# A decoder on one core: in differential attention the next group's projections enter the queue of filling work a batch earlier, with a second buffer for turned tokens and a third for queries and keys

## The chip, the cores and the metric

The kernel runs on one core of a Trainium2 chip. The metric is the time of one execution in device microseconds (us); the time before is the median of three runs. The core has five engines that run side by side, each through its own list of instructions in order: TensorE (PE: matmuls, and the loading of their weights, PEld), VectorE (DVE), ScalarE (ACT), GpSimd (POOL) and SyncE (SP), which here only issues transfers (DMA). Semaphores tie the engines together.

## The reference, cut to what matters

Six layers follow each other on 8 batches of 256 tokens of width 512, each with a residual and a layer norm: differential attention, a long convolution gated by a context, a mixture of experts, self attention, cross attention, routed attention. The change lies in the first; its end touches the second.

```python
q = (x @ Wq.T).reshape(bsz, tgt, 2 * H, HD)          # H = 16, HD = 16
k = (x @ Wk.T).reshape(bsz, tgt, 2 * KVH, HD)        # KVH = 4
v = (x @ Wv.T).reshape(bsz, tgt, KVH, 2 * HD)
scores = jnp.where(causal, einsum(q, k) * scale, min)
probs = jax.nn.softmax(scores, axis=-1)
attn = attn1 - lambda_full * attn2                   # even and odd heads of probs @ v
attn = attn * rsqrt(mean(attn * attn) + EPS) * ln_w * (1.0 - LAMBDA_INIT)
x = layernorm(x + attn.reshape(...) @ Wo.T)
```

## The kernel before, in words

The 2048 tokens are 16 tiles of 128 (`x[0]` to `x[15]`), and four tiles make a group: two batches. `causal_attention` (L1220) runs the attention of three of the layers; only `diff_attention` (L286) hands it a function `gather` and 8 units a batch (`upb = 8`, L561; the others take `upb = 4`). So differential attention is a loop of 64 **units**, 16 to a group (`upg`), each a block of four rows of heads of one batch.

A unit `u` issues, in this order (L1497 to L1521):

- `maxima(u)`: 12 matmuls for plain scores (`ps_q`, L1280), a copy by ACT (`rows`, L1289), a causal mask by POOL (L1291); the row maxima by DVE (L1300) come at the unit's end;
- some filling work;
- `products(u - 10)`: weights times values and times ones (`ps_pv`, L1386 and L1396), a reciprocal by DVE (L1404), then `gather`, which subtracts the odd heads (L428);
- `weights(u - 9)`: scores again, turned, with the maxima added by a second matmul (`ps_k`, L1343 and L1352), the exponential by ACT (`pT`, L1360), a mask and a sum by POOL (L1361, L1371);
- more filling work. Once a batch `split` and `turn` make the maxima into a matmul's operand (`terms` on DVE, L1311; `ps_n` on PE, L1322).

`ps_q` and `ps_k` share one buffer of PSUM (`ps_sc`, one buffer, L1240).

**Filling work** is everything else that PE has to do: turning tokens (`pt<-ident,x`, L226, to `xT`), the projections to values (`ps_v`), keys (`ps_k<-xT`, to `kz`) and queries (`ps_f`, to `qT`), the norm of the heads (`ps_ss`, `pt_ss`, `pt_rr`) and the output projection (`ps_o`, with `res` and the layer norm behind it); all projections carry line 207, a helper's. It stands in a list of pieces with a due slot each, with costs in us written beside every step (`MM, TR = 0.86, 0.45`, L201). `begin(g)` asks `prepare` (L351) for the pieces of group `g` and puts them in with due slots from `16 * g` on, where the group's first unit needs them. `fill(budget)` takes steps from the head of the list until the budget is spent; `need(u + 1)` takes all that is due, whatever the budget; the budget of a unit is

```python
rate = max(2.4, pressure(u) + per_batch / upb)
...
if u % upg == upb and u // upg + 1 < NG:
    begin(u // upg + 1)
left = fill(left + rate - short - MM) - need(u + 1)
```

so group `g + 1` enters at the middle of group `g`, eight units before it is due, at units 8, 24 and 40. When the list is empty, a unit gets no filling. `prepare` also starts, for the last group, the loads of the context's tiles (`cx`), which are turned from unit 54 on and written back as `ctx_d` (L423 to L424).

The tiles of this layer come from the pool `a_work` on the left side of the core's memory (SBUF): `qT` (8,192 bytes a partition) and `kz` (4,096) in two buffers, `xT` (8,192) in one. In the program as it is built the pool lies at bytes 91,136 to 196,256 of every partition. Two large tiles of the next layer lie at the right: `first_h` at 163,808 to 196,576, in memory that the pool leaves, and `w_l1a` at 196,576 to 229,344, above the pool's end. `long_conv` (L566) keeps in the lower half of `first_h` the turned even tiles of tokens and in the upper half their context; `w_l1a` holds the same of the odd tiles, which are first used at half of its 32 steps (`h`). It loads the context from `ctx_d` (L582), turns tokens (L171, copied out at L121 and L123), loads a filter a step (`wt`, three buffers, L596), and multiplies (`ps_y`, L177: 20 matmuls a step). At step 2 it issues the experts' weights (`gu`, L709), three transfers of 2,816 KB, into memory that the tokens of the first layer leave when the last of them is turned. Outside the attention loops the order of instructions is a scheduler's, which places them by data and memory.

Of the kernel before, what the change touches and what calls it, by code (L numbers as in the profile page):

```python
# [17 lines left out]
F32 = mybir.dt.float32  # L18
# [6 lines left out]
P = 128  # L25
# [3 lines left out]
NG = NT // TPG  # L29
GT = TPG * P  # L30
KB = D // P
# [21 lines left out]
def decoder_kernel(ctx: ExitStack, tc: tile.TileContext, a: dict, out: bass.AP):  # L53
# [149 lines left out]
    def by_columns(ps, lhsT, rhs, start, stop):  # L203

        for s in range(4):
            cs = slice(32 * s, 32 * s + 32)
            nc.tensor.matmul(ps[cs], lhsT=lhsT[:, cs], rhs=rhs, start=start, stop=stop)  # L207

    def product_steps(tile, lhsT, rhs, done, cost=MM):

        ps = []

        def step(k):
            if k == 0:
                ps.append(tile())
            by_columns(ps[0], lhsT(k), rhs(k), k == 0, k == KB - 1)
            if k == KB - 1:
                done(ps[0])

        return [(cost, lambda k=k: step(k)) for k in range(KB)]  # L220

    def turned(pools, dst, src, tag="mm"):

        pt = pools.tile([P, KB, P], F32, tag=tag, name="pt")
        for k in range(KB):
            nc.tensor.transpose(pt[:, k, :], src[:, k * P : (k + 1) * P], ident)  # L226
        nc.scalar.copy(dst, pt)  # L227
# [20 lines left out]
    def turned_group(work, pools, g, bufs=1):  # L248

        xT = []  # L250

        def step(ti):
            if ti == 0:
                xT.append(work.tile([P, KB, GT], F32, tag="xT", name="xT", bufs=bufs))
            turned(pools, xT[0][:, :, ti * P : (ti + 1) * P], x[g * TPG + ti])

        return xT, [(0, [(TR, lambda ti=ti: step(ti))]) for ti in range(TPG)]
# [28 lines left out]
    def diff_attention():  # L286
# [62 lines left out]
        clear_slots(wpool)  # L349

        def prepare(work, pools, g, at, here):  # L351
            qT = work.tile([P, KB, GT], F32, tag="qT", name="qT")
            kz = work.tile([P, 2, GT], F32, tag="kz", name="kz")
            v = work.tile([P, TPG, P], F32, tag="v", name="v", bufs=3)
            xT, turns = turned_group(work, pools, g)
            batches = [slice(b * S, (b + 1) * S) for b in range(2)]

            def values(ti, ps=[]):
                if ti == 0:
                    ps.append(pools.tile([P, TPG, P], F32, tag="mm", name="ps_v"))  # L360
                for k in range(KB):
                    by_columns(
                        ps[-1][:, ti, :],
                        xT[0][:, k, ti * P : (ti + 1) * P],
                        wv[:, k, :],
                        k == 0,
                        k == KB - 1,
                    )
                if ti == TPG - 1:
                    nc.scalar.copy(v, ps.pop())  # L370

            values_steps = [(MM, lambda ti=ti: values(ti)) for ti in range(TPG)]

            def keys(tokens):
                def done(ps):
                    for i in range(2):
                        nc.scalar.mul(kz[:, i, tokens], ps, half[:, i : i + 1])

                n = tokens.stop - tokens.start
                return product_steps(  # L380
                    lambda: pools.tile([P, n], F32, tag="mm", name="ps_k"),
                    lambda k: wk[:, k, :],
                    lambda k: xT[0][:, k, tokens],
                    done,
                    MM * n / GT,
                )

            if g:

                need = turns + [(0, values_steps), (0, keys(slice(0, GT)))]  # L390
            else:
                need = turns[:2] + [(0, keys(batches[0]))]
                need += [(3, steps) for _, steps in turns[2:]]
                need += [(8, keys(batches[1])), (9, values_steps)]
            for b, tokens in enumerate(batches):
                for c, first in enumerate((0, 1, 4, 5)):
                    block = feature_block(pools, qT, xT, wq, 0, c, HD0**-0.5, tokens)
                    need.append((8 * b + first, block))
            need.sort(key=lambda piece: piece[0])

            if g == NG - 1:

                for t in range(2):
                    load_context(work, t)
                for t in range(NT):
                    slot = 16 * g + 6 + t
                    at(slot - here, "fill", [(TR, lambda t=t: turn_context(work, pools, t))])
            return (
                need,
                lambda rows, c, at, n: qT[rows, c // 4 * 2 + c % 2, at : at + n],  # L410
                lambda rows, c, at, n: kz[rows, c // 2 % 2, at : at + n],
                lambda k, h: v[:, k, 32 * (h % 4) : 32 * (h % 4) + 32],
            )
# [3 lines left out]
        def load_context(work, t):  # L417
            cx[t] = work.tile([P, D], F32, tag="cx", name="cx")
            nc.sync.dma_start(out=cx[t], in_=cin[:, t, :])

        def turn_context(work, pools, t):
            c = work.tile([P, KB, P], F32, tag="cT", name="cT")
            turned(pools, c, cx.pop(t))  # L423
            nc.sync.dma_start(out=ctx_d[:, :, t * P : (t + 1) * P], in_=c)  # L424
            if t + 2 < NT:
                load_context(work, t + 2)
# [793 lines left out]
    def causal_attention(name, prepare, finish, upb=KB, gather=None):  # L1220
# [18 lines left out]
        with ExitStack() as st:  # L1239
            work = st.enter_context(tc.tile_pool(name=f"{name}_work", bufs=2))  # L1240
            ps_sc = st.enter_context(tc.tile_pool(name=f"{name}_sc", bufs=1, space=PSUM))
            ps_pv = st.enter_context(tc.tile_pool(name=f"{name}_pv", bufs=1, space=PSUM))
            pools = st.enter_context(tc.tile_pool(name=f"{name}_ps", bufs=3, space=PSUM))
# [168 lines left out]
            upg = 2 * upb  # L1412
# [21 lines left out]
            def happen(place):  # L1434
                for f in events.pop((now[0], place), []):
                    f()
# [18 lines left out]
            def begin(g):  # L1455
                pieces, *groups[g] = prepare(work, pools, g, at, now[0])
                queue.extend((upg * g + slot, steps) for slot, steps in pieces)
                queue.sort(key=lambda piece: piece[0])
# [14 lines left out]
            def pressure(u):  # L1473

                total = most = 0.0
                begun = [(due[0], current)] if current and due[0] < units + 99 else []
                for slot, steps in begun + queue:
                    total += sum(c for c, _ in steps)
                    most = max(most, total / max(1, slot - u))
                return most  # L1480
# [16 lines left out]
            for u in range(units + lag + 2):  # L1497
                now[0] = u
                happen("start")

                rate = max(2.4, pressure(u) + per_batch / upb)
                if u < units:
                    largest = maxima(u)
                    short = max(0.0, min(0.8, rate - 1.8))
                    if rate > 2.7:
                        short += (rate - 2.7) / 2
                    left = fill(left + short)
                    sums(u)
                    happen("mid")
                    if u >= wait:  # L1510
                        weights(u - wait)
                    if u % upg == upb and u // upg + 1 < NG:
                        begin(u // upg + 1)
                    left = fill(left + rate - short - MM) - need(u + 1)

                    if u and u % upb == 0:
                        turn(u // upb - 1)
                    left = fill(left + MM)
                    largest()
                    if u % upb == upb - 1:  # L1520
                        split(u // upb)  # L1521
                else:

                    if u < units + wait:
                        weights(u - wait)
                    sums(u)
                    happen("mid")
                    left = fill(left + rate) - need(u + 1)
                    if u == units:
                        turn(B - 1)  # L1530
                happen("end")
# [7 lines left out]
    def feature_block(pools, r, xT, w, at, c, scale=1.0, tokens=slice(0, GT)):  # L1539

        cs = slice(at + c * P, at + (c + 1) * P)
        n = tokens.stop - tokens.start
        return product_steps(
            lambda: pools.tile([P, n], F32, tag="mm", name="ps_f"),
            lambda k: w[:, k, cs],
            lambda k: xT[0][:, k, tokens],
            lambda ps: nc.scalar.mul(r[:, c, tokens], ps, scale),
            MM * n / GT,
        )
# [722 lines left out]
```

## Time and profile before

| what | value |
|---|---|
| median of 3 runs | 2106.0 us (2105.93 to 2106.16) |
| the profiled execution | 2125.86 us, its span 2124.1 us |
| PE busy over the span | 1946.4 us, 92% |
| DVE, POOL, ACT busy | 58%, 40%, 29% |
| differential attention | from the start to about 470 us: the last layer norm ends at 469.8 us |
| first unit, last unit (first `ps_q`) | 13.6 us, 391.4 us |
| long convolution, first `ps_y` | 480.1 us |

The profile is of one execution and slower than the median by 20 us; all times within a stage are read from it. In its timeline a row is a start, a duration, an engine, a line, an operation, output and inputs, shapes and a count, and in brackets how long the engine sat idle before it and what ended that. A matmul of the program is two rows of the trace here, since the numbers are in float32. The length of a unit is read as the time from its first `ps_q` to the next unit's.

### The profile page before, as it was taken

The numbers are of one execution on the slowest core, as the hardware profiler recorded it, in microseconds if no ns is written. First come the engines' busy times: TensorE is split into PE (matmuls) and PEld (weight loads), VectorE is DVE, ScalarE is ACT, GpSimd is POOL, SyncE is SP. The second block draws the span as 40 slices with busy tenths as digits, with TensorE's granted clock in tenths as the row PEclk, the third lists the DMA queues.
The fourth block names the chain that finished last, engine by engine and source line by source line (L and its number), as shares of the span: only waits on it lengthen the run. The fifth ranks groups of instructions, "written<-read, shape, count | busy, mean of one in ns | idle before, by whom it ended". The sixth has DMA issues, their size and how long they took to land. (4 is left out here: it accounts for less than half of the span.)

```text
span 2124.1 us, 46456 instructions
## 1 busy us (share of the span) xinstructions
PE 1946.4 (92%) x20164; PEld 1130.5 (53%) x20164; DVE 1234.4 (58%) x1890; ACT 615.2 (29%) x787; POOL 853.3 (40%) x945
## 2 busy tenths in 40 slices
PE   7979999879998999999969999998999999888885
PEld 5545545434443445566535554545877876254443
DVE  4677777658888974122226757556334342437877
ACT  4555555520010012111114343430101102144442
POOL 2677777637556823000015645343000000216663
PEclk9999999999999999999989999999999999999997
DMA  6899924235124135132122311002000000250000
GB/s 228 321 398 390 383 82 92 81 90 205 30 72 152 49 118 184 64 124 86 50 85 77 101 30 63 3 2 100 31 20 30 31 10 1 100 173 14 24 24 31
DMA packets 141628, 220.29 MB, mean 104 GB/s; under 512 B 27440, under 2 KB 56240, under 8 KB 141424
## 3 DMA queue, kind: packets, MB, share of 16 engines
q1 hardware_dynamic: 134960, 196.97, 26.7%
q0 software_dynamic: 6464, 20.32, 2.8%
q8 instruction: 161, 2.64, 0.5%
q14 instruction: 43, 0.35, 0.1%
HBM read 106.51 MB, written 123.34 MB: 108 GB/s over the span
## 5 line engine op out<-in xcount | busy, mean ns | idle before, releaser
L1404 DVE RECIPROCAL rsum<-ps_pv 128x256 f32<-128x256 f32 x128 | 224.6, 1755 | 229.3 <-PE ps_pv L1396 229.2
L177 PE MATMUL ps_y<-kv,wt 128*128 128x512 f32 x640 | 279.0, 594 | 5.9 <-DVE kv L602 2.7
L1360 ACT ACTIVATE pT<-ps_k 128x1536 f32<-128x1536 f32 x128 | 185.7, 1451 | 252.8 <-PE ps_k L1352 229.7
L1300 DVE TENSOR_REDUCE neg<-rows 128x12 f32<-128x1536 f32 x128 | 222.9, 1742 | 53.3 <-POOL rows L1291 53.2
L1289 ACT COPY rows<-ps_q 128x1536 f32<-128x1536 f32 x128 | 184.1, 1438 | 164.8 <-PE ps_q L1280 107.0
L1361 POOL TENSOR_SCALAR_AFFINE_SELECT pT<-pT 128x1024 f32<-128x1024 f32 x128 | 141.4, 1105 | 193.8 <-ACT pT L1360 193.8
L1291 POOL TENSOR_SCALAR_AFFINE_SELECT rows<-rows 128x1024 f32<-128x1024 f32 x128 | 141.6, 1106 | 174.1 <-ACT rows L1289 173.6
L177 PEld LDWEIGHTS ps_y<-kv,wt 128*128 128x128 f32 x640 | 120.0, 190 | 156.9 <-issue 136.4
L1371 POOL TENSOR_TENSOR pT<-pT 128x512 f32<-128x512 f32 x112 | 147.0, 1313 | 9.3
L1199 POOL DMA_INDIRECT w_l1x<-ys,slots x32 | 33.4, 1043 | 265.4 <-DMA ys<-y_m 257.8
L207 PE MATMUL ps_f<-xT,w_l1a 128*32 128x256 f32 x2048 | 123.3, 384 | 1.1 <-ACT xT L227 1.1
L1396 PE MATMUL ps_pv<-pT,ones_v 128*32 128x256 f32 (+1 forms) x1152 | 88.4, 387 | 14.1 <-POOL pT L1371 14.0
L1107 PE MATMUL po_m<-dn,hT 128*128 (+1 forms) x216 | 98.7, 593 | 1.0 <-ACT hT L1097 1.0
L145 POOL TENSOR_SCALAR rstd<-bn_mv 128x1 f32<-128x1 f32 x80 | 16.7, 208 | 205.8 <-DVE bn_mv L151 199.6
L640 DVE TENSOR_REDUCE yc<-z 128x64 f32<-128x512 f32 x128 | 86.2, 674 | 5.6 <-POOL w_l1a L641 5.2
L207 PEld LDWEIGHTS ps_f<-xT,w_l1a 128*32 128x32 f32 x2048 | 62.3, 110 | 46.9 <-issue 8.7
L1280 PE MATMUL ps_q<-kT,qT 32*128 32x128 f32 x1536 | 63.6, 297 | 21.5 <-ACT pT L1360 15.8
L1280 PEld LDWEIGHTS ps_q<-kT,qT 32*128 32x128 f32 x1536 | 51.0, 194 | 59.0 <-ACT pT L1360 24.8
L1280 PE MATMUL ps_q<-kz,qT 32*128 32x128 f32 x1536 | 62.2, 292 | 16.8 <-ACT pT L1360 13.4
L177 PE MATMUL pg<-gu,xT_b 128*128 x216 | 72.3, 471 | 4.6 <-issue 3.7
L1280 PEld LDWEIGHTS ps_q<-kz,qT 32*128 32x128 f32 x1536 | 49.8, 190 | 45.4 <-ACT pT L1360 31.6
L1343 PE MATMUL ps_k<-qT,kT 32*128 32x256 f32 (+1 forms) x1024 | 69.3, 357 | 4.8 <-ACT pT L1360 2.5
(374 smaller groups left out, 3585.3 us busy)
## 6 DMA issues: line engine op xcount, KB each, us to landing
xs<-zero SPq DMA_DIRECT2D x8, 4352.0 KB
ys<-zero SPq DMA_DIRECT2D x8, 4352.0 KB
filters<-in_L_xattn_k SPq DMA_DIRECT2D x4, 2560.0 KB
first_h<-xs SPq DMA_DIRECT2D x36, 256.0 KB
ys<-y_m SPq DMA_DIRECT2D x36, 256.0 KB
gu<-in_L_ffn_gate_up_proj SPq DMA_DIRECT2D x3, 2816.0 KB
wt<-filters SPq DMA_DIRECT2D x32, 256.0 KB
sorted_x<-zero SPq DMA_DIRECT2D x1, 5120.0 KB
```

Source lines behind the costliest of these rows:

```text
L177: nc.tensor.matmul(ps, lhsT=lhsT(k), rhs=rhs(k), start=(k == 0), stop=(k == n - 1))
L207: nc.tensor.matmul(ps[cs], lhsT=lhsT[:, cs], rhs=rhs, start=start, stop=stop)
L1107: nc.tensor.matmul(po, lhsT=hT[:m, i, :], rhs=dn[i][:m, bass.ds(e, 1), :], start=(i == 0), stop=(i == len(FCH) - 1),)
L1280: nc.tensor.matmul(block[:, s, j, :], lhsT=q(rows, c, b * S + i * P, P), rhs=k(rows, c, b * S + keys * P, P), start=True, stop=True,)
L1289: nc.scalar.copy(d.rearrange("p j s k -> p s j k"), block)
L1291: nc.gpsimd.affine_select(out=rows, in_=rows, compare_op=ALU.is_ge, fill=-FAR, base=0, pattern=[[0, 8], [-1, P]], channel_multiplier=1,)
L1300: return lambda: nc.vector.tensor_reduce(neg[u // upb % 2][:, :, :, c], d, AX.X, ALU.max, negate=True)
L1360: nc.scalar.activation(p[:, 0:3].rearrange("p j s q -> p s j q"), block, AF.Exp)
L1361: nc.gpsimd.affine_select(out=p[:, 0:2].rearrange("p j s q -> p (j s) q"), in_=p[:, 0:2].rearrange("p j s q -> p (j s) q"), compare_op=ALU ...
L1371: nc.gpsimd.tensor_tensor(p[:, 3], p[:, 1], p[:, 2], ALU.add)
L1396: nc.tensor.matmul(ps[32 * s : 32 * s + 32, 1, j * P :], lhsT=ones_v, rhs=p[:, 1, s, :] if j else first[:, :, s, :], start=(j == 0), stop= ...
L1404: nc.vector.reciprocal(r, ps[:, 1, :])
```

## The change

`begin` moves from the middle of a group to its start where a `gather` is given, which is differential attention alone: units 0, 16 and 32 in place of 8, 24 and 40. The due slots stay. So that the earlier work has where to go, `xT` gets a second buffer, `qT` and `kz` a third; `v` had three. The loads of the first context tiles are issued with the last `begin`, eight units earlier as well.

```diff
@@ -349,10 +349,10 @@
         clear_slots(wpool)
 
         def prepare(work, pools, g, at, here):
-            qT = work.tile([P, KB, GT], F32, tag="qT", name="qT")
-            kz = work.tile([P, 2, GT], F32, tag="kz", name="kz")
+            qT = work.tile([P, KB, GT], F32, tag="qT", name="qT", bufs=3)
+            kz = work.tile([P, 2, GT], F32, tag="kz", name="kz", bufs=3)
             v = work.tile([P, TPG, P], F32, tag="v", name="v", bufs=3)
-            xT, turns = turned_group(work, pools, g)
+            xT, turns = turned_group(work, pools, g, bufs=2)
             batches = [slice(b * S, (b + 1) * S) for b in range(2)]
@@ -1509,7 +1509,7 @@
                     if u >= wait:
                         weights(u - wait)
-                    if u % upg == upb and u // upg + 1 < NG:
+                    if u % upg == (0 if gather else upb) and u // upg + 1 < NG:
                         begin(u // upg + 1)
                     left = fill(left + rate - short - MM) - need(u + 1)
```

## The prediction, written before the changed kernel was run

> **What bounds the kernel now.** I read the page first (PE busy 92%), then the waits inside differential attention (0 to 440 us), the timeline of PE unit by unit, and the timeline of SP across its end. The waits, as waiter, awaited, total us, times, longest:
>
> ```profile
> ACT pT L1360 <- PE ps_k L1352: 112.3, 59, 4.4
> DVE rsum L1404 <- PE ps_pv L1396: 91.9, 51, 3.8
> ACT rows L1289 <- PE ps_q L1280: 50.2, 52, 2.2
> POOL pT L1361 <- ACT pT L1360: 47.5, 31, 3.6
> ```
>
> The reader sees a ring, not one full engine: each engine waits for the one before it. A unit without filling shows the ring's length (PE, unit 20):
>
> ```profile
> 114.25 0.95 PE L1280 MATMUL ps_q<-kz,qT 32*128 32x128 f32 x24 [1.63 <-ACT pT L1360]
> 115.85 0.86 PE L1386 MATMUL ps_pv<-pT,v 128*32 128x256 f32 x16 [0.64 <-POOL pT L1361]
> 117.20 0.64 PE L1396 MATMUL ps_pv<-pT,ones_v 128*32 128x256 f32 x8 [0.50 <-POOL pT L1371]
> ...
> 120.50 0.95 PE L1280 MATMUL ps_q<-kz,qT 32*128 32x128 f32 x24 [1.63 <-ACT pT L1360]
> ```
>
> PE is idle 2.77 us of 6.25: exponential, POOL's mask and sum, PE's sums, next scores, exponential. The other extreme is unit 48 (293.8 to 303.8, 10.0 us), where the last group's projections fall due:
>
> ```profile
> 298.76 2.78 PE L207 MATMUL ps_o<-w_l,yT_b 128*32 128x512 f32 x24
> 301.36 1.91 PE L207 MATMUL ps_f<-xT,w_l 128*32 128x256 f32 x32
> 303.09 0.29 PE L1322 MATMUL ps_n<-ident_b,terms 128*32 128x128 bf16 x8
> 303.78 0.95 PE L1280 MATMUL ps_q<-kz,qT 32*128 32x128 f32 x24 [0.39 <-ACT qT L1547]
> ```
>
> Here PE's filling stands ahead of the next scores. So a unit costs the ring, or PE, whichever is longer.
>
> **The change, part by part.**
>
> *The units.* No matmul is added or removed. I priced the filling from PE's timeline, start to start: a step of `ps_f` 0.43 us, of `ps_k` or `ps_o` 0.93, a tile of `ps_v` 1.0, a turned tile 0.59, `ps_ss` 0.6, `pt_ss` 0.4. With each program's order of instructions this gives the filling between one `ps_q` and the next:
>
> ```
> unit          7   8  17  18  19  20  21  23  26  35  48  50  51  52  53  54  56
> before, us  1.3 2.5 1.7 1.0 0.0 0.0 0.6 1.5 3.6 2.2 5.5 2.3 2.6 2.6 2.3 3.4 3.5
> after, us   2.5 3.3 3.4 3.0 2.9 2.3 2.2 3.2 1.9 3.6 2.8 2.3 0.0 0.0 0.6 2.5 2.6
> ```
>
> Both sum to 148.2 us over units 0 to 62; units 0 to 6 and 59 to 62 are the same. The empty stretch moves from units 18 to 21 to units 51 to 53; the clump at 48 goes. To price that I set the length of units 9 to 62 (26 left out, see below) against their filling. Under 2.4 us the length doesn't follow it (means 6.03, 5.99 for under 1.1, 1.1 to 2.2); a line through all 53 gives 5.98 us plus 1.13 for each us over 2.4. The filling over 2.4 sums to 15.8 us before and 12.8 after: 3.0 x 1.13 = **3.4 us gained**.
>
> *Unit 26* took 10.1 us where that line says 7.3. Its rows: three copies of `xT` (1.56 us) and the square of `yT_b` (1.06) stand on ACT ahead of `rows`, which starts 2.65 us after `pT` ends where 1.07 is usual (unit 20): 1.6 late. Then PE runs at half speed from 155.8 to 159.2. After, the turning of group 2 falls in unit 17 and the square in 18: two copies and the square (2.2 us) ahead of `rows`, 1.1 late. Bounds: all of the 2.75 goes, or none. I take 1.6, all but the 1.1 that ACT still costs, since the half-speed spell follows PE's wait in this unit: **1.6 us gained**.
>
> *Unit 8* (6.74 us): PE idles 2.95 us until DVE's `terms` at 46.3, then turns two tiles before `ps_q` at 48.1. After, two turned tiles and one tile of `ps_v` stand inside that idle time, one tile of `ps_v` (1.0) behind `ps_n`: `ps_q` at about 47.4. **0.7 gained**; bounds 0 and 2.0, the filling moved out.
>
> *Buffers and waits.* I price these at nothing. Without a second `xT`, turning group 2 in unit 17 would wait for the last `ps_f` of group 1, issued in the same unit. `qT` and `kz` of group g are read until unit 16g + 24, group g + 2 writes from 16g + 17: three live at once. The tokens `x` of group 1 are wanted in unit 7 in place of 8; their issue ends at 23.4 us and the turning at 42.25 doesn't wait for them. The earlier `cx` loads stand on SP behind the zeroing of `xs` and `ys` as before, and are read at unit 54.
>
> *The end of the layer.* The buffers add 8,192 x 2 + 4,096 = 20,480 bytes, so `a_work` ends at 216,736: over the lower part of `w_l1a`, which was free. What SP and PE do there now:
>
> ```profile
> 432.68 3.79 SPq L582 DMA_DIRECT2D w_l1a<-ctx_d  x4
> ...
> 469.97 3.94 SPq L582 DMA_DIRECT2D first_h<-ctx_d  x4
> 473.96 23.91 SPq L596 DMA_DIRECT2D wt<-filters  x5
> 501.84 7.15 SPq L709 DMA_DIRECT2D gu<-in_L_ffn_gate_up_proj  x3
> ```
>
> ```profile
> 480.08 17.43 PE L177 MATMUL ps_y<-kv,wt 128*128 128x512 f32 x40 [0.46 <-DMA wt<-filters]
> 497.35 1.04 PE L171 MATMUL pt<-ident,x 128*128 128x128 f32 x8
> ...
> 501.15 0.66 PE L171 MATMUL pt<-ident,x 128*128 128x128 f32 x4 [1.91 <-DVE w_l1a L123]
> ```
>
> Half of the context is fetched at 432 us, hidden under the attention. In the changed program it comes after `first_h`'s half and ahead of the first filter, and waits for the memory of `res`, last read by the layer norm at 469.8. `first_h` no longer overlaps `res`; its last old tenant is `yT_b`, read until 466.4, so its half starts 3.5 us earlier. A half's packets (2 MB) take 7.2 us (471.1 to 478.3), the filters 0.7 each. So: 467.5 + 7.2 + 7.2 + 0.7 + 1.1 from packets to PE (as now) = `ps_y` at 483.7 in place of 480.1, **3.6 us lost**. Against that the three late turnings (0.87, 0.49), the idle 1.91 before one and `ps_cs` (0.81), now among the `ps_y`, all come before the first: 4.1 us regained. PE has them done by about 482, since DVE's first copy still stands behind the last layer norm. Net **0.5 gained**; bounds 2.0 gained (the filters come in time, turnings alone set the start), and, lost, 3.6 with nothing regained plus 3.5 if the early start of `first_h` fails: 7.1. The experts' weights start some 18 us sooner, at 484, and take 20.7 us (504 to 525 now), so the fourth filter lands at about 506 and is wanted at 483.7 + 3 x 8.7 = 510. From 484 on the convolution keeps PE full, so what is gained stays.
>
> *The sum.* 3.4 + 1.6 + 0.7 + 0.5 = 6.2 us. Against the profiled execution's 2125.86 us that is 2119.7; against the median, 2106.0 - 6.2 = **2099.8 us** (0.3%), taken over because the ring and the clock spells stand in stages that repeat.
>
> **A rule weighed.** The granted clock was 0.83 in 120 to 130 us, after the empty units: `ps_pv` took 1.51 us for 0.86, sums and `ps_k` 1.0 more. One such spell costs about 1.7 us, less what the ring hides. I let the spell at 122 go and one come at units 51 to 53, for nothing. The Trainium skill ("TensorE: Matmul & The Clock Gate", section "HAM oscillation — how this bites in real kernels") says that PE throttles after a gap of over some 3.4 us. The trace differs: the longest gap before 122 is 1.63 us. By the page no empty unit would cost a spell before or after, and the sum would be the same.
>
> **The rivals.**
>
> *The empty stretch only moves* (within 0.2%): the two ACT-heavy units meet in 17 and 18 at full price, the spells swap, and the 1.13 holds for the clump at 48 alone, the heavier units 17, 18, 23, 35 paying some back. For it: equal sums of filling. Against: unit 48 is 4 us over the ring. It gives 1 to 3 us: about 2104.
>
> *The context blocks the filters* (slower): if `first_h` isn't released early, `ps_y` starts at 487.2, 7.1 us late; with DVE behind after the late start, the 4.1 us aren't regained. It decides once the delay exceeds the 5.7 us of the units, and is over the bound only if these give under 3: 7.1 - 2.5 = 4.6 lost, about 2110.6. For it: the filter is what `ps_y` waits for already. Against: DVE and POOL have the first products ready earlier.
>
> *The change doesn't do what it says*, the early work waiting on PE for copies by ACT, falls into the first rival.
>
> **How the numbers follow.** About 0.2% (4.2 us) is what a measurement can tell from no change. The forecast's own case (2095.5 to 2101.8) has 0.60, the empty stretch that only moves (2101.8 to 2107.5) 0.29, the blocked filters 0.11, nearly all slower. The low end adds the open bounds of units 8 and 26 and of the turnings (1.1 + 1.3 + 1.5, rounded up). The range, 2095.5 to 2107.5, leaves out the third case and the first one's tail.
>
> **What would show it.** Right: units 17 to 23 with `ps_v`, `ps_k`, `ps_f` in them at about 6 us; unit 48 near 6.5; units 51 to 53 with PE idle over 2 us; last `ps_q` some 6 us earlier; `w_l1a<-ctx_d` issued after `first_h<-ctx_d`; `ps_y` 3 to 4 us further behind the last layer norm, and unbroken after it. Wrong: units 17 to 25 at 6.5 us or more, a half-speed spell in them, or a stall of `ps_y` at its fourth filter.

## The result, and the profile after

The changed kernel takes **2116.1 us** in the median of 11 runs (2111.2 to 2117.6), the kernel before beside it 2106.6 (11 runs, 2102.6 to 2110.9). The ratio is 1.0039, 95% interval 1.0029 to 1.0050 (the medians alone give 1.0045): some 8 us slower (6.1 to 10.5), where 6.2 us faster was forecast. The profiled execution of the changed kernel took 2115.25 us, its span 2113.6. That of before was 20 us over its median, and where the two executions differ most is behind the convolution (1347.4 us from the last `ps_y` to the end, 1328.8 after, in work that the change doesn't touch), so stages are compared here, not spans.

The waits inside differential attention (0 to 440 us), the same four lines as before:

```profile
ACT pT L1360 <- PE ps_k L1352: 105.0, 57, 3.4
DVE rsum L1404 <- PE ps_pv L1396: 93.3, 50, 4.0
ACT rows L1289 <- PE ps_q L1280: 55.7, 53, 3.2
POOL pT L1361 <- ACT pT L1360: 49.6, 32, 3.6
```

The ring is still the ring: ACT waits for the turned scores 7 us less (in unit 48 itself 2.7 us as before), and for the plain ones (`ps_q`) 5.5 us more. These sums don't say who is late. PE's own waits do, between the first `ps_q` of unit 9 and of unit 63; of before, then of after:

```profile
PE ps_q L1280 <- ACT pT L1360: 13.4, 12, 1.6
...
PE pt_ss L522 <- DVE means L516: 1.1, 3, 0.5
```

```profile
PE ps_q L1280 <- ACT pT L1360: 11.2, 9, 1.6
...
PE pt_ss L522 <- DVE means L516: 5.1, 4, 2.0
...
PE pt L226 <- DVE yT_b L554: 2.8, 1, 2.8
PE ps_q L1280 <- issue: 1.7, 1, 1.7
```

The wait that belongs to the ring shrank a little (13.4 to 11.2 us). New are waits of filling work for DVE, and a stop of 1.7 us that has no releaser. Unit 20, which was empty, is now full and quicker (5.71 us for 6.25), and unit 48 is no clump any more (7.40 for 9.99). Their rows, from the unit's first `ps_q` to the next unit's:

```profile
119.46 0.95 PE L1280 MATMUL ps_q<-kz,qT 32*128 32x128 f32 x24
120.34 1.07 PE L207 MATMUL ps_k<-xT,w_l 128*32 128x512 f32 x8
...
125.17 0.95 PE L1280 MATMUL ps_q<-kz,qT 32*128 32x128 f32 x24 [0.20 <-ACT pT L1360]
```

```profile
301.90 0.95 PE L1280 MATMUL ps_q<-kz,qT 32*128 32x128 f32 x24
...
306.90 0.64 PE L207 MATMUL ps_f<-xT,w_l 128*32 128x256 f32 x8
307.36 1.04 PE L207 MATMUL ps_o<-w_l,yT_b 128*32 128x512 f32 x8
308.21 0.29 PE L1322 MATMUL ps_n<-ident_b,terms 128*32 128x128 bf16 x8
308.32 1.04 PE L207 MATMUL ps_o<-w_l,yT_b 128*32 128x512 f32 x8
309.30 0.95 PE L1280 MATMUL ps_q<-kz,qT 32*128 32x128 f32 x24
```

At the end of the layer, SP's queue has the order that the prediction named: both halves of the context, then the filters.

```profile
469.79 3.87 SPq L582 DMA_DIRECT2D first_h<-ctx_d  x4
473.82 7.17 SPq L582 DMA_DIRECT2D w_l1a<-ctx_d  x4
481.03 2.68 SPq L596 DMA_DIRECT2D wt<-filters  x3
487.22 5.97 SPq L709 DMA_DIRECT2D gu<-in_L_ffn_gate_up_proj  x3
```

What PE did meanwhile, up to the first product with a filter:

```profile
481.19 0.66 PE L171 MATMUL pt<-ident,x 128*128 128x128 f32 x4 [0.68 <-ACT w_l1a L121]
483.41 1.99 PE L171 MATMUL pt<-ident,x 128*128 128x128 f32 x12 [1.56 <-DVE w_l1a L123]
486.07 1.12 PE L171 MATMUL pt<-ident,x 128*128 128x128 f32 x4 [0.68 <-ACT w_l1a L121]
488.17 1.88 PE L177 MATMUL ps_cs<-rw,ones_m 128*128 128x8 f32 x8 [0.98 <-DVE w_l1a L123]
489.90 40.37 PE L177 MATMUL ps_y<-kv,wt 128*128 128x512 f32 x87
```

No row here waits for a filter: `ps_y` starts right behind turnings and sums (`ps_cs`) that wait for copies of the turned odd tiles by DVE and ACT. DVE's queue shows why they are late:

```profile
479.46 3.29 DVE L602 TENSOR_TENSOR kv<-first_h 128x512 f32<-128x512 f32 x3
482.68 1.28 DVE L123 COPY w_l1a<-pt 128x512 f32<-128x512 f32 x2
...
485.17 2.02 DVE L602 TENSOR_TENSOR kv<-first_h 128x512 f32<-128x512 f32 x2
487.11 0.40 DVE L618 TENSOR_REDUCE us<-u 128x32 f32<-128x256 f32 x1
487.44 1.27 DVE L123 COPY w_l1a<-pt 128x512 f32<-128x512 f32 x2
```

The copies stand behind the products of tokens and context (`kv`) of the even tiles. In the table, and below, the end of the layer is counted from one mark, the end of the second-last normalisation (`x<-res`, L160, DVE; 468.55 us before, 471.87 after):

| from the mark | before | after | forecast |
|---|---|---|---|
| to the first `ps_y` | 11.5 | 18.0 | 15.2 |
| first 20 rows of `ps_y` (one step) | 8.7 | 11.5 | 8.7 |
| next 40 | 20.6 | 17.2 | |
| the rest | 267.3 | 266.3 | |
| mark to the last `ps_y` | 308.1 | 312.9 | 307.6 |

(Forecast: 483.7 - 468.55 = 15.2, and 308.1 - 0.5.) The layer's end lost 4.8 us in this execution, and the units 9 to 62 took 346.0 us where before they took 343.3.

### The profile page after: what moved, and what is told of

Same layout as the page of the kernel before. It is cut to its first block, busy times and chain, and to the rows that moved or that the text cites. A ratio compares the mean times of both kernels' runs of the same rounds, so it can differ in the third digit from the quotient of the medians.

```text
span 2113.6 us, 46455 instructions
## 1 busy us (share of the span) xinstructions
PE 1943.7 (92%) x20164; PEld 1126.6 (53%) x20164; DVE 1244.9 (59%) x1890; ACT 615.6 (29%) x787; POOL 851.6 (40%) x945
## 5 line engine op out<-in xcount | busy, mean ns | idle before, releaser
L1280 PE MATMUL ps_q<-kz,qT 32*128 32x128 f32 x1536 | 61.3, 287 | 15.1 <-ACT pT L1360 11.2
L1086 DVE TENSOR_TENSOR h_b<-h_b,pg 128x352 f32<-128x352 f32 x36 | 18.8, 521 | 92.5 <-ACT h_b L1085 92.5
```

The lines of the kernel that those rows point to most:

```text
L1280: nc.tensor.matmul(block[:, s, j, :], lhsT=q(rows, c, b * S + i * P, P), rhs=k(rows, c, b * S + keys * P, P), start=True, stop=True,)
```

## The experiments

Two things in the change can be separated: the **buffers**, which move SP's order, and the **earlier begin**, which moves filling between units. My theory after the result: the buffers cost about 4 us at the end of the layer, because the context's odd half goes ahead of the filters; the earlier begin costs some 3 to 4 us more in the units, since its pieces end up behind DVE at new places. Rivals: the loss is chance between executions, or all of it is in one of the two. Each ratio is against runs of the kernel before on the same chip; those took 2127.9 to 2129.8 us in the median there.

**No edit.**

> The kernel before, unchanged, for a second profile. All theories: no difference in time (ratio 1.000). What it tells is how far two profiles of one kernel differ by stage: the first unit started at 13.6 us before and at 16.2 after, where both programs are the same. If that is run-to-run, this profile's first unit lies anywhere between 13 and 17 us, and the length of units 9 to 62 within 2 us of 343.3.

Measured: ratio 1.0000 (0.9986 to 1.0015). Units 9 to 62 took 345.0 us, mark to last `ps_y` 309.2. What one profile tells of the units is good to a us or two.

**The buffers alone.**

```diff
-  if u % upg == (0 if gather else upb) and u // upg + 1 < NG:
+  if u % upg == upb and u // upg + 1 < NG:
```

> The buffers of the change without the early begin: in the attention the order of instructions on every engine is that of before, and SP's order after it is that of the changed kernel. Memory theory (the pool's growth over w_l1a puts half of the context ahead of the first filter, and that costs the time): first ps_y some 6 us further behind the last layer norm than before, of which 4 to 5 stay; time 4 to 6 us over before (ratio 1.002 to 1.003), units 9 to 62 as before. Filling theory (the early filling itself is what is slower): time as before (within 1 us), all of the 8 to 9 us lie between this kernel and the changed one.

Measured: 1.0019 (1.0005 to 1.0034). The units are those of before (342.9 us), and the end of the layer is that of after: first `ps_y` 17.3 us behind the mark, 311.2 to the last, 2.6 over the mean of the kernels with the order of before (308.5). So the buffers alone cost about 4 us by the ratio (1 to 7), and the profile shows the loss at the layer's end.

**The change again.**

> The changed kernel, unchanged, beside the others on one chip. Ratio 1.004 to before by the result. Memory theory: 3 to 4 us over e2, no gain from the filling. Filling theory: 8 to 9 us over e2. My forecast's arithmetic of the units: 5.7 us under e2. Its profile tells whether the long units 32, 36 and 42 (9.3, 8.6, 9.2 us) come again: a wait of the order of instructions would, a stall of a moment would not.

Measured: 1.0048 (1.0031 to 1.0065). Units 9 to 62: 348.2 us; mark to last `ps_y`: 312.1. The loss is no chance.

**The change, with the context's odd half fetched behind the first filters.** Step 16 is the first to read it; step 6 now fetches it.

```diff
-            for i in range(2):
+            def context(i):
...
+            context(0)
...
+                if h == 6:
+                    context(1)
```

> The changed kernel with the odd tiles' half of the context fetched at step 6 of the convolution's code in place of before its first step; SP then issues the first three filters ahead of it. Memory theory: first ps_y 3 us after the turnings are done, at most 10 us behind the last layer norm's end as before, time 4 to 6 us under the changed kernel (1.001 to 1.002 to before). Filling theory: time as the changed kernel.

Measured: 1.0014 (0.9999 to 1.0028). The first `ps_y` is 12.0 us behind the mark and the last 306.3: the layer's end is no longer later than before, but 2 us sooner. Against the change itself, run beside it on the same chip (1.0031 to 1.0065), the intervals don't touch: the place of these four loads is worth some 7 us there. Units 9 to 62 still take 347.1 us.

**The same and the begin one unit later** (units 1, 17, 33), which puts other pieces beside each other.

```diff
-  if u % upg == (0 if gather else upb) and u // upg + 1 < NG:
+  if u % upg == (1 if gather else upb) and u // upg + 1 < NG:
```

> e4 with the early begin one unit later, at units 1, 17 and 33. The filling over 2.4 us sums to 12.1 us in place of 12.8, so the load theory gives 1 us under e4. In the order of instructions no tokens are turned behind pt_rr any more (unit 32), and the square sums follow an output block's end in one unit (50) in place of two (34, 42). Queue theory: units 32, 33 and 42, 43 near 6.2 us each, together 8 to 10 us less than in e4, some of it lost at unit 50: time 5 to 8 us under e4, 2 to 5 us under before.

Measured: 1.0001 (0.9987 to 1.0014). Units 9 to 62 take 343.6 us, and the two longest new units are gone: 32 and 33 take 6.98 and 6.01 us, 42 and 43 take 6.77 and 6.19. The gain hoped for didn't come: in unit 49 the output projection now waits 1.59 us for DVE (`yT_b`, L554), PE goes at a clock of 0.56 for 3.5 us behind that wait, and the unit takes 9.0 us; the empty unit 52 takes 8.2. It is as fast as before, not faster.

**The means of the squares by ACT in place of DVE**, on the fourth kernel, on the begin one unit later, and on the kernel before.

```diff
-  nc.vector.tensor_scalar(means, ps, 1.0 / 32, EPS, ALU.mult, ALU.add)
+  nc.scalar.mul(means, ps, 1.0 / 32)
...
-  nc.vector.tensor_copy(
+  nc.vector.tensor_scalar(
...
+      EPS,
+      None,
+      ALU.add,
```

> e4 (the changed kernel, odd half of the context fetched late) with the means of squares copied out of PSUM by ACT in place of DVE; the small constant is added one step later, on the 128x32 copy. Queue theory (the early filling lost because PE, in order, now stands behind DVE's queue: pt_ss behind means 5.1 us against 1.1 before, the turning at unit 32 behind pt_rr's reader 2.8 us): the waits of pt_ss fall to about 1 us, unit 42 from 9.2 to about 6.5 and unit 43 with it, since the half-speed spell after the wait goes; units 9 to 62 shorter by 4 to 6 us, time 4 to 6 us under e4, that is at or a little under the kernel before. Load theory (early filling makes units longer by its amount, 1.13 us for each over 2.4): no change to e4.

> e6 and e5 together. Queue theory: no long unit left but the clump's remains; the shortest of all, 1 to 2 us under e6, 4 to 7 us under before (ratio 0.997). Load theory: as e6.

> The kernel before with the means on ACT, nothing else. Both theories: 0 to 1 us under before, since pt_ss waits for means 1.1 us in all there. If it gains as much as e5 gains over e4, the copy's place helps for a reason of its own and e5 says nothing of the early filling.

Measured: 1.0002 (0.9989 to 1.0015), 0.9994 (0.9982 to 1.0005) and 0.9993 (0.9981 to 1.0004). Each is 0.7 to 1.2 thousandths under its parent, with intervals that overlap (and 0.3 under the later repeat of the fourth kernel): **inconclusive** in time. The 4 to 6 us expected of the first didn't come: its units 9 to 62 take 348.1 us, 0.9 more than in the fourth kernel. Unit 42 did fall, from 9.2 to 7.8 us, and 43 from 7.5 to 5.9, but 32 and 33 keep their length (9.7 and 8.1), and units 37, 53, 54 and 61 are 0.7 to 1.6 us longer. The second has the shortest units of all, 341.2 us, in one profile and without a difference in time that can be told; the third takes 343.9. In the trace the wait changed hands more than it went. PE's wait before `pt_ss` in the first of the three, to set beside the 5.1 us above:

```profile
PE pt_ss L522 <- ACT means L516: 3.7, 4, 1.3
```

On the kernel before, the same wait grew, from 1.1 us to 2.7.

No version beats the kernel before by more than a measurement can tell.

**The context late without the earlier begin, and with it again**, on one chip, to separate the two parts once more. The first is the second experiment with the edit of the fourth, the second is the fourth unchanged.

> The buffers alone, with the later half of the context fetched behind the first filter: the order of the filling is that of before. If the 4 us of the buffers alone (ratio 1.0019) come from the context's place in the queue, the first product with the filters starts some 12 us after the mark in the last layer norm (11.7 before, 17.3 with the buffers alone), units 9 to 62 take 343 to 345 us, and the ratio to before is 0.9990 to 1.0007. If the buffers cost something else (the larger pool, other addresses), the start comes back and the ratio stays at 1.0015 or more.

> The change with the later half of the context behind the first filter, again, beside the run without the earlier begin: the two differ only in the unit at which a group's projections enter the filling. If the earlier begin itself costs what the units show (3 to 4 us over units 9 to 62), this run is 2 to 5 us longer than the other; if the units' loss is made good later, the two are equal within 1 us. If the earlier begin gains as forecast (5.7 us), it is shorter by that.

Measured: 1.0002 (0.9990 to 1.0015) and 1.0005 (0.9995 to 1.0015). The first settles the buffers in their stage: the buffers are the same, only the place of four loads on SP changed, and the layer's end goes from 311.2 to 306.3 us. In time it is as fast as before; its interval overlaps that of the buffers alone. SP and PE in it:

```profile
466.46 3.86 SPq L582 DMA_DIRECT2D first_h<-ctx_d  x4
470.37 2.69 SPq L598 DMA_DIRECT2D wt<-filters  x3
473.16 6.44 SPq L582 DMA_DIRECT2D w_l1a<-ctx_d  x4
```

```profile
480.04 0.66 PE L171 MATMUL pt<-ident,x 128*128 128x128 f32 x4 [1.56 <-DVE w_l1a L123]
480.53 17.33 PE L177 MATMUL ps_y<-kv,wt 128*128 128x512 f32 x40
```

The same wait for DVE's copy is there (1.56), but three turnings and `ps_cs` no longer stand before the first `ps_y`. The second of the two did not come out as the theory said: 1.0 us under the first by the medians and 0.6 over it by the ratios, where 2 to 5 over was expected. Its units show the loss, 347.3 us against 345.9 (in this execution of the first, units 20 and 61 took 1.1 and 1.5 us more than in before's profile), but the measured time doesn't resolve it.

The executions side by side, in us:

| | units 9 to 62 | mark to first `ps_y` | first 20 `ps_y` | mark to last `ps_y` | ratio |
|---|---|---|---|---|---|
| before | 343.3 | 11.5 | 8.7 | 308.1 | 1 |
| before again | 345.0 | 11.7 | 8.7 | 309.2 | 1.0000 |
| buffers alone | 342.9 | 17.3 | 10.4 | 311.2 | 1.0019 |
| buffers, context late | 345.9 | 12.0 | 8.6 | 306.3 | 1.0002 |
| after | 346.0 | 18.0 | 11.5 | 312.9 | 1.0039 |
| after again | 348.2 | 17.4 | 10.2 | 312.1 | 1.0048 |
| after, context late | 347.1 | 12.0 | 8.6 | 306.3 | 1.0014 |
| the same again | 347.3 | 12.1 | 8.6 | 307.1 | 1.0005 |

The earlier begin costs 3.0 us in the units: a mean of 347.2 over the last four rows, and 344.2 over the four rows above them and the last kernel of the means (343.9). In time it costs 5.2 us with the context early (the mean of 1.0039 and 1.0048, less 1.0019, of 2106.6) and 1.6 with it late (the mean of 1.0014 and 1.0005, less 1.0002), each uncertain by 3 us or more. That it doesn't gain the 5.7 us forecast is shown; whether in time it costs next to nothing or 5 us stays open.

## Why the prediction was wrong, point by point

**The end of the layer: forecast 0.5 gained, measured about 4 lost** (312.5 in the mean of the two executions of the changed kernel, 308.5 in that of the three with the order of before: these two and the means by ACT, 308.2). The transfers went nearly as forecast: `first_h`'s half is issued 2.1 us before the mark where it was issued 1.4 behind it, the packets of the two halves take 470.9 to 485.9 us (15.0, where 14.4 was forecast), and the first filter's last packet ends at 486.3, so that `ps_y` could have begun at about 487.2 (0.9 behind it, as before). The mark is 3.3 us later than before, so that is 483.9 on before's clock, where 483.7 was forecast. The step that failed is "PE has them done by about 482, since DVE's first copy still stands behind the last layer norm". The odd tiles' turnings need DVE's copies one after another, and two groups of `kv` stand between these; the last turning and `ps_cs` were done at 489.9, 486.6 on before's clock. I had followed the transfer and PE, and of DVE's queue only its first copy.

So, as one sum: the forecast start 3.6 later, 2.9 more for DVE's queue and PE's clock, 2.8 more for the first 20 `ps_y`, less 4.5 regained later (3.4 in the next 40, 1.0 in the rest): 4.8. The 4.1 us of turnings did come back, a little later and in full; the 2.9 and the 2.8 were not in the sum. In the two other executions with this order they are 2.1 to 2.2 and 1.6 to 1.7. The second is PE's clock, and so is part of the first (`ps_cs` took 1.88 us here, 1.06 with the buffers alone), in the windows of 482 to 486, 486 to 490 and 490 to 494 us:

```profile
482.00:486.00 4.00, 1.91 (x12) 1.25 (x12) 4.00 (x7) 1.15 (x2) 3.92 (x5) 0.91 1.20 298
486.00:490.00 4.00, 2.94 (x13) 2.55 (x13) 2.97 (x6) 0.02 (x1) 4.00 (x6) 0.50 0.80 244
490.00:494.00 4.00, 4.00 (x6) 1.73 (x6) 1.76 (x5) 0.00 (x0) 3.92 (x7) 0.50 1.03 415
```

The columns are the window's length, the busy time of PE, PEld, DVE, ACT and POOL (with the number of rows), the granted clock, the share of the DMA engines and GB/s. PE, idle half of the first window, goes at half speed through the next two, into the convolution. With the buffers and the context late PE's clock is 1.00 from 478 us on.

**The units: forecast 5.0 gained in units 9 to 62 (3.4 by the line, 1.6 at unit 26), measured 3.0 lost.** The failed step is the line itself, "5.98 us plus 1.13 for each us over 2.4": it prices how much filling a unit holds, and not what the filling waits for. The filling moved just as the table of the prediction has it, and where a unit's length did come from the amount, the forecast held. Lengths of units before and after, means over the executions (the first five are those with the old begin, the other four those with the new one):

```
unit      8    20    26    40    48  |   32    33    42    43    36
old    6.84  6.85  9.97  7.66  9.99  | 7.41  5.69  6.55  6.48  6.35
new    5.57  5.72  6.13  6.50  7.41  | 9.49  7.43  9.22  7.09  7.64
```

On the left units 26 and 48 alone give 6.4 us back (3.8 of it unit 26, whose own term was 1.6); units 17 to 23, forecast at about 6, take 5.7 to 6.9. On the right 32, 33, 42 and 43 take 7.1 us more, and 36 another 1.3. Together that is 2.0 of the 3.0 lost; the other 1.0 is the sum of many units that gain or lose up to 1.2 each. Three mechanisms stand behind the right side.

The first is a wait for DVE, and it repeats in all four executions. In unit 32 (of after) the second turning of tokens wants the buffer of PSUM that is next in turn of three, and `pt_rr` holds it until DVE has multiplied by it (L554):

```profile
199.87 0.66 PE L226 MATMUL pt<-ident,x 128*128 128x128 f32 x4
203.28 0.66 PE L226 MATMUL pt<-ident,x 128*128 128x128 f32 x4 [2.76 <-DVE yT_b L554]
203.87 0.95 PE L1280 MATMUL ps_q<-kz,qT 32*128 32x128 f32 x24
```

```profile
198.90 0.68 DVE L262 TENSOR_TENSOR res<-ps_o,x 128x512 f32<-128x512 f32 x1
...
200.45 1.73 DVE L1404 RECIPROCAL rsum<-ps_pv 128x256 f32<-128x256 f32 x1
202.21 0.42 DVE L433 TENSOR_TENSOR yT_b<-ps_pv,rsum 128x256 f32<-128x256 f32 x1
202.55 0.68 DVE L554 TENSOR_TENSOR yT_b<-yT_b,pt_rr 128x512 f32<-128x512 f32 x1
```

DVE is never idle here. The turning waits 2.76 us for it, and `ps_q`, which wants nothing of either, waits behind the turning on PE. In unit 42 the same happens with `means`: an output block now ends just before the squares are summed, so `res` and its statistics stand on DVE ahead of `means`, and `pt_ss` waits 1.97 us (0.21 before) with `ps_q` behind it. Begun one unit later, both places are clean, and a wait for DVE of the same kind is in unit 49; with the means on ACT, unit 42 falls and unit 32 does not. These experiments show the cause to be the neighbourhood of the pieces. Which single neighbour would do at unit 32 wasn't tried.

The second effect is the clock again. Units 33 and 43 hold no more filling than others (2.7 us each, by the rows), but in three of the four executions they take about 7.5 to 8.2 us, at half speed for a part of it. In unit 43 of the last experiment, behind a wait of 1.97 us:

```profile
268.10:275.50 7.40, 7.40 (x121) 4.22 (x120) 3.97 (x6) 3.07 (x3) 4.00 (x6) 0.77 1.01 382
```

In the changed kernel's own profile the same wait is followed by a clock of 1.00 and a unit of 5.9 us. So a spell after such a wait came in six of eight cases, and cost 1.6 to 2.4 us each time. The prediction let one spell go and one come, "for nothing"; units 51 to 53 did get theirs (0.72 in 333 to 339 us), and 33 and 43 came on top. The Trainium skill ("TensorE: Matmul & The Clock Gate", section "A second HAM failure mode: psum-queue depth-cycling") tells of throttling that comes from many short idles. The waits here are single ones of 2.0 and 2.8 us: shorter than the one long gap of the rule which the prediction weighed, and no run here shows that they are the page's short idles.

The third is in unit 36, where PE stops after six of 24 `ps_q`, at the same place in all four executions (1.70, 1.37, 1.68 and 1.64 us), with no engine that it waits for. The traces point to the supply of PE's own instructions. The queue that they mark as "instruction" moves 16 KB at a time, once for some 250 rows of PE and PEld (161 times in all), and one such transfer starts at 222.83 us, 2.43 before PE goes on at 225.26. So it is with every stop of PE of over 0.3 us without a releaser up to 480 us: 20 in the twelve profiles, each 2.2 to 2.5 us behind the start of such a transfer, while these start some 8 us apart. That is read from the times; no experiment moved it.

**Unit 8: forecast 0.7 gained, measured 1.3** (6.84 to 5.57): right in kind, but unit 7, which took over filling and was in no term, is 0.8 longer (2.51 to 3.34), so the pair gains 0.4.

The three stages together: 4.0 and 3.0 us lost, 0.4 gained, so 6.6 lost, inside the measured 6.1 to 10.5.

**Buffers, `cx` loads, waits for memory: forecast nothing.** No such wait for SBUF is in the trace of after; right, apart from SP's order, which was a term of its own.

**The rivals.** That the empty stretch "only moves" was true of the filling but no rival in time; what it said of the heavier units paying back did come (17, 23 and 35 are 0.5, 0.8 and 1.1 us longer). "The context blocks the filters" named the right place and the wrong condition: it made the loss depend on `first_h` not being released early, which it was, and on DVE being behind "after the late start". DVE was behind before it. The forecast gave that side 0.11; the weight should have followed from the odd tiles' copies standing on DVE with `kv` between them, and from a gain in units that rested on sums of filling alone.

## What to carry to other kernels

Where one engine works its queue in order, moving work is priced by its new neighbours: for each moved piece, find whose buffer or result it needs, what stands ahead of that on the other engine, and what critical instruction stands behind the piece. A sum of busy time doesn't see any of it. And a pool that grows can change the order of transfers far away: look for the tiles that its new bytes cover, and follow the next stage's start through every engine that feeds it, not through the transfer alone.

## What the runs showed of the hardware

- Most lengths of units repeat to 0.01 or 0.02 us over executions and chips (unit 48: 9.99 to 10.00 in five, 7.40 to 7.42 in four), although the whole differs by 1% between chips. Those that don't are mostly units with a half-speed spell in some executions (unit 20: 6.25 us at a clock of 1.00, 7.58 at 0.65). A per-unit table from single profiles can be trusted more than the span.
- DVE's three `kv` in a row took 1.97 us before, with POOL idle (0.00 busy in 474 to 478 us), and 3.29 after, with POOL busy for 3.20 of the 3.30 us. The Trainium skill ("SBUF — State Buffer", section "SBUF: two separate sides") says that an operation of VectorE with two inputs in SBUF and one of GpSimd that reads SBUF lock each other out for a whole instruction. The rows fit that; it wasn't tried alone, and nothing in the prediction priced it.
- The context's transfers ran at 290 GB/s, the experts' weights behind them at 415, on the same engines. The first go in packets of 512 bytes, the second in packets of 2,816.
